# A graph layer on one Trainium2 core: aggregation by seven half-size products, and node loops in a written order

## The chip, the core and the metric

The kernel runs on one core of a Trainium2 chip. The core has five engines that run side by side: TensorE (PE, matrix products, with a weight loader of its own, PEld), VectorE (DVE), ScalarE (ACT), GpSimd (POOL) and SyncE (SP, which here only issues transfers). Each works through its own list of instructions in order and waits on semaphores for the others. TensorE writes its products to PSUM, eight banks of 128 x 512 fp32 numbers; VectorE and ScalarE read them from there; everything else lives in SBUF, and DMA moves data between SBUF and memory. The metric is the time of one execution on the device in microseconds (us), less being better.

## What is computed

For 32 graphs (batches) of 512 nodes with 256 features each, and a 0/1 matrix `adj` of 512 x 512 for each graph, one layer of a gated graph network, all in fp32:

```python
h = jnp.maximum(_layernorm(x), 0.0)
xc = jnp.transpose(h, (0, 2, 1))
t = relu(bn1(conv1d(xc, conv1_w)))               # 1 tap: a matrix product
t = bn2(conv1d(t, conv2_w, pad=8))               # 17 taps, 256 x 256 channels
x_conv = relu(t + xc).transpose(0, 2, 1)
s = h @ w_se.T + b_se                            # 3 numbers a node
A = jnp.exp(-squared_distance(s, s)) * adj
msg = relu(h @ w_msg.T + b_msg)
x_nmp = jnp.einsum('bnm,bmd->bnd', A, msg)       # the aggregation
gi = concatenate([x_conv, x_nmp]) @ w_ih.T + b_ih
gh = h @ w_hh.T + b_hh
r, z = sigmoid(gi_r + gh_r), sigmoid(gi_z + gh_z)
n = tanh(gi_n + r * gh_n)
out = x + (1 - z) * n + z * h
```

`A` is symmetric, since `adj` is.

## The kernel before

The batches are worked on in two groups (`g`) of 16. For each group `first_part` normalises, transposes (h goes to memory as `HD`), applies the 1-tap convolution and takes windows of 80 tokens to the frequency domain (`xf`). The 17-tap convolution is done there as 40 products by frequency, called units (`u`): unit 0 holds the two real frequencies, every other unit a complex number for each of 128 windows and 256 channels, times a 256 x 256 complex matrix. `load_unit` fetches the two matrices of a unit (`WT`, three buffers), `prepare` makes the sums that a complex product by three real ones needs (on GpSimd), and `product` multiplies, closes the sums and stores the result to memory (`YD`).

The function `nodes` follows each group's first part. It loops over the 16 batches of the group and does, for each, the following:

- `by_chunks` reorders h (ScalarE), `message` multiplies it by the message weights together with the three projection columns (TensorE; bias on VectorE, relu on ScalarE), `features` makes the small vectors from which a squared distance is one product (VectorE), `factors` transposes them (TensorE, copies by ScalarE).
- `affinity` multiplies the factors (tile `pd`), takes the exponent (`e`, ScalarE), transposes the 0/1 matrix in 32 x 32 blocks (`at`, VectorE) and multiplies the two into `A` (VectorE).
- `aggregate` multiplies the messages by `A`: two banks of 128 x 512 (tile `pn`), each a sum over four blocks of 128 nodes. ScalarE copies them to `nmp`, and `save_nmp` stores them to memory (`ND`).

The units are spread over the loop to fill TensorE: 36 of group 0 over its 16 iterations (two, two, two, three, and so on; the last four go into the first part of group 1), 40 of group 1 over the first 13 iterations (three each, four in the last). An iteration works ahead: it aggregates batch i, makes messages of batch i+2 and the affinity of batch i+1.

A late stage then reads HD, ND and YD back, takes the convolution back from the frequency domain (constant `back`, made on the host) and computes the gates. It takes about 965 us and isn't touched but for numbers in `back`. It already computes its gate products by seven half-size products out of sums that GpSimd makes (`sums`, tiles `hp`, `np`, `cp`).

The order of instructions on each engine is the order of the program text inside `tc.manual_schedule()`. Outside, a scheduler orders them by priority as they become ready in its own model of time. In `nodes` only the opening lines (988 to 993) stand inside such a block; the loop over the batches (995 to 1022) is left to the scheduler. Buffers are taken from pools, where tiles with one tag share `bufs` slots, and a new tile waits for the last reader of the one whose slot it takes. PSUM is one such pool of eight banks.

An fp32 product appears in the profile as two matmul instructions: the eight products of one aggregation are sixteen MATMULs.

Of the kernel before, what the change touches and what calls it, by code (L numbers as in the profile page):

```python
# [15 lines left out]
P = 128  # L16
# [14 lines left out]
def dft_constants(taps, tokens):  # L31
# [16 lines left out]
    back[2::2], back[3::2] = 2 * cos.T, -2 * sin.T  # L48
# [17 lines left out]
def gnn_layer(  # L66
# [42 lines left out]
    XP, HP, NP, CP, YT, RZ, NT, OUT = ({} for _ in range(8))  # L109
# [252 lines left out]
    def prepare(pw, g, u, xf):  # L362
        if (g, u) not in WT:
            load_unit(g, u)
        if u > 0:
            if (g, u) not in WSUM:
                sum_unit(pw, g, u)
            re, im = factors_of(xf, u)
            both = BOTH[g, u] = pw.tile([P, 2, DC, P], FP, tag="both", name=f"both_{g}_{u}", bufs=2)
            nc.gpsimd.tensor_tensor(both[:, 0], re, im, op=ALU.add)  # L370
            nc.gpsimd.tensor_tensor(both[:, 1], im, re, op=ALU.subtract)

    def product(pw, g, u, xf):
# [11 lines left out]
        else:  # L385
            both, wsum = BOTH.pop((g, u)), WSUM.pop((g, u))
            k3 = bank(f"py2_{g}_{u}")[:, :D]
            terms = [(k3, both[:, 1], wr), (k2, both[:, 0], wi), (k1, re, wsum)]
# [7 lines left out]
        else:  # L396
            nc.scalar.copy(y_im, halves(k1))  # L397
            nc.vector.tensor_sub(y_re, y_im, halves(k2))  # L398
            nc.vector.tensor_add(y_im, y_im, halves(k3))
        nc.scalar.dma_start(YD[g][:, 2 * u : 2 * u + 2, :], y)  # L400
# [67 lines left out]
    def affinity(b):  # L468
# [7 lines left out]
        for mc in range(NC):  # L476
            e = pools["nodes"].tile([P, N], FP, tag="e", name=f"e_{b}_{mc}", bufs=2)
            nc.scalar.activation(e, pd[mc], AF.Exp)  # L478
            at = pools["nodes"].tile([P, N], FP, tag="at", name=f"at_{b}_{mc}", bufs=2)
            nc.vector.transpose(at.rearrange("p (j k) -> p j k", k=32), ADJ[b][:, :, 32 * mc : 32 * (mc + 1)])  # L480
            nc.vector.tensor_mul(A[b][:, mc, :], e, at)  # L481
        del ADJ[b]

    def aggregate(b, dcs=range(DC)):
        if 0 in dcs:
            NMP[b] = work.tile([P, DC, N], FP, tag="nmp", name=f"nmp_{b}")
        for dc in dcs:
# [5 lines left out]
        if DC - 1 in dcs:  # L493
            del MSG[b], A[b]
# [441 lines left out]
    with tc.tile_pool(name="freq", bufs=1) as fpool:  # L936
# [36 lines left out]
        def nodes(g, xf, units, last):  # L973


            b1 = (g + 1) * GB
            todo = [b1 - 1] + list(range(g * GB, b1 - 1))
            def begin(i):
                if i < GB:
                    if todo[i] not in HQ:  # L980
                        by_chunks(todo[i])
                    message(todo[i])
                    features(todo[i])

            load_adj(todo[0])
            if (g, 2) not in WT:
                load_unit(g, 2)
            with tc.manual_schedule():
                begin(0)
                message(todo[1], [0])  # L990
                factors(todo[0])
                message(todo[1], [1])
                features(todo[1])
            affinity(todo[0])
            for i, b in enumerate(todo):
                mine = spread(units, i, last) if i < last else []
                more = i + 1 < GB
# [3 lines left out]
                if g + 1 < NG and i == 3 * GB // 4:  # L1001
                    statistics(b1)
                if more:
                    load_adj(todo[i + 1])
                    factors(todo[i + 1])

                parts = [range(DC)] if mine or not more else [[0], [1]]
                if len(parts) > 1:
                    aggregate(b, parts.pop(0))
                for u in mine[:1]:  # L1010
                    product(pools["pw"], g, u, xf)
                begin(i + 2)
                if i + 3 < GB:
                    load_h(todo[i + 3])
                if more:
                    affinity(todo[i + 1])
                for u in mine[1:2]:
                    product(pools["pw"], g, u, xf)
# [108 lines left out]
```

## Time and profile before

| | before |
|---|---|
| time, median of 3 runs | 1830.86 us (1827.69 to 1835.83) |
| span of the profiled execution, first to last instruction | 1830.0 us |
| time of the profiled execution beyond its span | not given apart |
| PE busy | 1815.0 us (99%) |
| DVE, ACT, POOL busy | 1107.4, 583.8, 588.6 us |
| loop of group 0 | about 157 to 460 us of the span |
| loop of group 1 | about 565 to 865 us |
| late stage | about 865 to 1830 us |

A group of instructions in the profile is one line of the kernel on one engine: the tiles written and read, the shape, the count, then busy time in us and the mean of one in ns, then the idle time of the engine ahead of it and what ended it. A timeline line gives the start in us, the length, the engine, the line and the tiles; "x16" stands for sixteen instructions merged. In a table of stretches, each engine has its busy time and its instructions.

### The profile page before, as it was taken

To read this page: it belongs to the slowest core of one execution; us is meant where nothing else is said; L and a number is where in the kernel's file an instruction comes from. 1 tells how busy PE (TensorE), PEld (TensorE's weight loads), DVE (VectorE), ACT (ScalarE), POOL (GpSimd) and SP (SyncE) were. 2 spreads that over 40 slices of the span, in tenths; PEclk is the share of its full clock that TensorE was granted. 3 is DMA by queue.
4 is the path that set the end of the run, shared out by engine and by line. 5 is a ranking of instruction groups with operands and counts; after the bars stand their busy time and mean duration, and the time that the engine had idled before them with its cause. 6 is when DMAs were issued, how large, how long until landed. Compare 5 with 4: busy or idle time off the path is not lost.

```text
span 1830.0 us, 20109 instructions
## 1 busy us (share of the span) xinstructions
PE 1815.0 (99%) x6614; PEld 1083.9 (59%) x6614; DVE 1107.4 (61%) x2220; ACT 583.8 (32%) x1084; POOL 588.6 (32%) x569
## 2 busy tenths in 40 slices
PE   9999999999999999999999999999999999999998
PEld 6777666666997766765545554555445554555444
DVE  7884565655995555554266556654665466645666
ACT  4555443432345343333212221222122221222121
POOL 3431333334432443444321332123221323133221
PEclk9999999999999999999999999999999999999999
DMA  9998989775669987767332344224422443234412
GB/s 252 307 297 220 254 225 263 192 197 190 214 218 226 262 242 226 237 187 256 93 108 57 77 121 121 78 44 121 121 87 35 120 121 98 51 93 121 114 23 54
DMA packets 308652, 289.26 MB, mean 158 GB/s; under 512 B 148076, under 2 KB 238732, under 8 KB 308164
## 3 DMA queue, kind: packets, MB, share of 16 engines
q1 hardware_dynamic: 282964, 225.79, 46.4%
q10 hardware_dynamic: 18992, 38.68, 5.9%
q0 software_dynamic: 6592, 23.50, 4.1%
q8 instruction: 53, 0.87, 0.2%
q14 instruction: 51, 0.42, 0.1%
HBM read 191.50 MB, written 96.40 MB: 157 GB/s over the span
## 4 chain that ended last, share of the span: by engine, by line
PE 65%; issue 1%; DVE 1%; POOL 1%; ACT 0%; DVEq 0%; POOLq 0%; ACTq 0%
PE pg L600 30%; PE pn L600 15%; PE pn L490 6%; PE py L391 6%; PE pc L588 5%; PE pm L438 2%; PE pd L475 1%; PE pz L600 1%; PE psr L464 0%; DVE A L481 0%; POOL cp L578 0%; POOL nt L791 0%; POOL rz L790 0%; DVE at L480 0%; DVE o L671 0%
## 5 line engine op out<-in xcount | busy, mean ns | idle before, releaser
L490 PE MATMUL pn<-A,msg 128*128 128x512 f32 x512 | 225.6, 593 | 0.9 <-DVE A L481 0.9
L600 PE MATMUL pg<-hp,sw 128*128 128x512 f32 x434 | 221.8, 593 | 0.7 <-DVE rz L619 0.5
L600 PE MATMUL pg<-np,sw 128*128 128x512 f32 x434 | 221.6, 592 | 0.0
L600 PE MATMUL pg<-cp,sw 128*128 128x512 f32 x434 | 221.6, 592 | 0.0
L578 POOL TENSOR_TENSOR hp<-hp 128x512 f32<-128x512 f32 x64 | 81.3, 1281 | 413.1 <-DMA hp<-hd 352.0
L370 POOL TENSOR_TENSOR both<-xf 128x256 f32<-128x256 f32 x78 | 60.1, 770 | 319.1 <-PE py L391 283.7
L490 PEld LDWEIGHTS pn<-A,msg 128*128 128x128 f32 x512 | 96.9, 190 | 111.0 <-issue 105.8
L578 POOL TENSOR_TENSOR cp<-cp 128x512 f32<-128x512 f32 x64 | 80.5, 1268 | 229.8 <-ACT cp L594 228.6
L391 PE MATMUL py<-wt,both 128*128 128x256 f32 x624 | 151.0, 384 | 0.5 <-ACT e L478 0.5
L615 ACT ACTIVATE rz<-rz,brz 128x512 f32<-128x512 f32 x93 | 67.0, 721 | 260.2 <-DVE rz L619 260.2
L398 DVE TENSOR_TENSOR y<-y,py 128x256 f32<-128x256 f32 x78 | 31.8, 407 | 188.5 <-ACT y L397 186.3
L600 PEld LDWEIGHTS pg<-hp,sw 128*128 128x128 f32 x434 | 82.2, 190 | 104.7 <-issue 97.3
L600 PEld LDWEIGHTS pg<-cp,sw 128*128 128x128 f32 x434 | 82.5, 190 | 103.8 <-issue 103.8
L600 PEld LDWEIGHTS pg<-np,sw 128*128 128x128 f32 x434 | 82.5, 190 | 103.8 <-issue 103.8
L391 PEld LDWEIGHTS py<-wt,both 128*128 128x128 f32 x624 | 113.9, 190 | 43.6 <-issue 27.6
L481 DVE TENSOR_TENSOR A<-e,at 128x512 f32<-128x512 f32 x128 | 115.7, 942 | 29.5 <-ACT e L478 29.3
L357 POOL TENSOR_TENSOR wsum<-wt 128x512 f32<-128x512 f32 x78 | 109.7, 1407 | 56.1 <-DMA wt<-wd 42.9
L739 ACT ACTIVATE nt<-nt,vech 128x512 f32<-128x512 f32 x64 | 46.2, 722 | 235.8 <-DVE nt L738 235.8
L326 PE MATMUL pc<-w,hT 128*128 128x256 f32 x512 | 118.9, 386 | 0.8 <-DVE hT L314 0.8
L438 PE MATMUL pm<-wmsg,hq 128*128 128x259 f32 x512 | 117.5, 381 | 0.0
L600 PE MATMUL pn<-cp,sw 128*128 128x512 f32 x224 | 114.4, 592 | 0.0
L600 PE MATMUL pn<-hp,sw 128*128 128x512 f32 x224 | 114.4, 592 | 0.0
(145 smaller groups left out, 2945.8 us busy)
## 6 DMA issues: line engine op xcount, KB each, us to landing
wt<-wd SPq DMA_DIRECT2D x160, 256.0 KB, 4.3
adj<-in_adj_dram SPq DMA_DIRECT2D x128, 256.0 KB, 5.4
wd<-wst SPq DMA_DIRECT2D x64, 320.0 KB, 5.9
yd<-y ACTq DMA_DIRECT2D x80, 256.0 KB, 3.9
yt<-yd SPq DMA_DIRECT2D x30, 640.0 KB, 7.5
hd<-hT SPq DMA_DIRECT2D x32, 512.0 KB, 5.0
nd<-nmp ACTq DMA_DIRECT2D x32, 512.0 KB, 4.5
xb<-in_x_dram SPq DMA_DIRECT2D x128, 128.0 KB, 3.7
```

The costliest lines, as they stand in the source:

```text
L326: nc.tensor.matmul(p[:, j, :], HT[b][:, ic, c * P : (c + 1) * P], w1[:, ic, :], start=(ic == 0), stop=(ic == DC - 1))
L357: nc.gpsimd.tensor_tensor(t, WT[g, u][:, 0], WT[g, u][:, 1], op=ALU.add)
L370: nc.gpsimd.tensor_tensor(both[:, 0], re, im, op=ALU.add)
L391: nc.tensor.matmul(dst, v[:, ic, :], w[:, ic, :], start=(ic == 0), stop=(ic == DC - 1))
L438: nc.tensor.matmul(p[:, : D + NS], hq[:, ic, c * P : (c + 1) * P], wmsg[:, ic, :], start=(ic == 0), stop=(ic == DC - 1))
L481: nc.vector.tensor_mul(A[b][:, mc, :], e, at)
L490: nc.tensor.matmul(p, MSG[b][:, mc, dc * P : (dc + 1) * P], A[b][:, mc, :], start=(mc == 0), stop=(mc == NC - 1))
L578: nc.gpsimd.tensor_tensor(t[:, dst, :], t[:, a, :], t[:, b, :], op=sub)
L588: nc.tensor.matmul(bk[:, t0:t1], YT[p][j][:, c, oc * P : (oc + 1) * P], back[:, n : n + t1 - t0], start=(c == 0), stop=(c == len(spans) - ...
L600: nc.tensor.matmul(bk[:, t], sw[:, k, q, o, :], terms[k][q][:, t], start=(first and i == 0), stop=(i == len(ks) - 1), skip_group_check=True)
L615: nc.scalar.activation(rz[:, g, j, :], src, AF.Sigmoid, bias=brz[:, g : g + 1], scale=1.0)
L739: nc.scalar.activation(n, n, AF.Tanh, bias=b_in[:, i : i + 1], scale=1.0)
```

## The change

**Aggregation.** For batches with `i <= last` (all 16 of group 0, the first 14 of group 1) `aggregate7` replaces `aggregate`. The 256 x 512 by 512 x 512 product is cut into 2 x 2 blocks and done by seven half-size products of sums instead of eight (Strassen's scheme in Winograd's form). Each is four MATMUL of 256 columns over two contraction blocks, twice for fp32. The sums of `A`'s blocks (`affinity_sums`, tile `ts`) and of the messages' blocks (`message_sums`, tile `ms`) are made by GpSimd, four instructions each. Three PSUM banks are used; products accumulate into a bank after ScalarE has copied what stood there, and VectorE closes the four output blocks with five additions.

**Affinity.** `affinity` becomes three functions: `turn` (the transposes), `exponents` (the exponent goes straight to `A`, without `e`), and `masked` (the multiplication, in place).

**Complex products.** `prepare` makes one sum of the data (`re + im`) instead of a sum and a difference. ScalarE writes one product twice, once multiplied by -2, so that the stored second part is imaginary minus real; `back` is changed to match. The order of the three terms is turned around, and the store can be put off (`later`).

**Order.** Both calls of `nodes` stand wholly in `tc.manual_schedule()`. Loads of units follow the products, 0/1 matrices are loaded two batches ahead, and stores of products are collected and issued by `flush`.

**Buffers.** `nmp` one instead of two; `e` goes; `ts` and `ms` one each; `p7` two; `both` half as large.

```diff
-    back[2::2], back[3::2] = 2 * cos.T, -2 * sin.T
+    back[2::2], back[3::2] = 2 * (cos - sin).T, -2 * sin.T
...
-            both = BOTH[g, u] = pw.tile([P, 2, DC, P], FP, tag="both", name=f"both_{g}_{u}", bufs=2)
-            nc.gpsimd.tensor_tensor(both[:, 0], re, im, op=ALU.add)
-            nc.gpsimd.tensor_tensor(both[:, 1], im, re, op=ALU.subtract)
+            both = BOTH[g, u] = pw.tile([P, DC, P], FP, tag="both", name=f"both_{g}_{u}", bufs=2)
+            nc.gpsimd.tensor_tensor(both, re, im, op=ALU.add)
...
-            terms = [(k3, both[:, 1], wr), (k2, both[:, 0], wi), (k1, re, wsum)]
+            terms = [(k1, re, wr), (k2, im, wi), (k3, both, wsum)]
...
-            nc.scalar.copy(y_im, halves(k1))
-            nc.vector.tensor_sub(y_re, y_im, halves(k2))
+            nc.scalar.copy(y_re, halves(k1))
+            nc.scalar.mul(y_im, halves(k1), -2.0)
+            nc.vector.tensor_sub(y_re, y_re, halves(k2))
             nc.vector.tensor_add(y_im, y_im, halves(k3))
-        nc.scalar.dma_start(YD[g][:, 2 * u : 2 * u + 2, :], y)
+        store = partial(nc.scalar.dma_start, YD[g][:, 2 * u : 2 * u + 2, :], y)
...
+    def turn(b, mcs):
+        for mc in mcs:
+            at = AT[b, mc] = pools["nodes"].tile([P, N], FP, tag="at", name=f"at_{b}_{mc}", bufs=2)
+            nc.vector.transpose(at.rearrange("p (j k) -> p j k", k=32), ADJ[b][:, :, 32 * mc : 32 * (mc + 1)])
...
-            e = pools["nodes"].tile([P, N], FP, tag="e", name=f"e_{b}_{mc}", bufs=2)
-            nc.scalar.activation(e, pd[mc], AF.Exp)
...
-            nc.vector.tensor_mul(A[b][:, mc, :], e, at)
+            nc.scalar.activation(A[b][:, mc, :], pd[mc], AF.Exp)
+
+    def masked(b, mcs):
+        for mc in mcs:
+            nc.vector.tensor_mul(A[b][:, mc, :], A[b][:, mc, :], AT.pop((b, mc)))
+
+    H = N // 2
+
+    def quads(t, width):
+        return [t[:, 2 * k : 2 * k + 2, width * j : width * (j + 1)] for k in range(2) for j in range(2)]
+
+    def affinity_sums(b):
+        b11, b12, b21, b22 = quads(A[b], H)
+        t = TS[b] = pools["nodes"].tile([P, 3, 2, H], FP, tag="ts", name=f"ts_{b}", bufs=1)
+        sub = ALU.subtract
+        nc.gpsimd.tensor_tensor(t[:, 0], b22, b12, op=sub)
+        nc.gpsimd.tensor_tensor(b12, b12, b11, op=sub)
+        nc.gpsimd.tensor_tensor(t[:, 1], b22, b12, op=sub)
+        nc.gpsimd.tensor_tensor(t[:, 2], b21, t[:, 1], op=sub)
+
+    def message_sums(b):
+        a11, a21, a12, a22 = quads(MSG[b], P)
+        t = MS[b] = pools["nodes"].tile([P, 3, 2, P], FP, tag="ms", name=f"ms_{b}", bufs=1)
+        sub = ALU.subtract
+        nc.gpsimd.tensor_tensor(t[:, 0], a11, a21, op=sub)
+        nc.gpsimd.tensor_tensor(a21, a21, a22, op=ALU.add)
+        nc.gpsimd.tensor_tensor(t[:, 1], a21, a11, op=sub)
+        nc.gpsimd.tensor_tensor(t[:, 2], a12, t[:, 1], op=sub)
...
+    def aggregate7(b):
+
+        m11, s1, m12, m22 = quads(MSG.pop(b), P)
+        b11, t1, b21, b22 = quads(A.pop(b), H)
+        (s3, s2, s4), (t3, t2, t4) = ([t[:, n] for n in range(3)] for t in (MS.pop(b), TS.pop(b)))
+        nmp = NMP[b] = work.tile([P, DC, N], FP, tag="nmp", name=f"nmp_{b}", bufs=1)
+        c11, c12, c21, c22 = (nmp[:, i, H * j : H * (j + 1)] for i in range(2) for j in range(2))
+        p1 = pools["nodes"].tile([P, H], FP, tag="p7", name=f"p7_{b}", bufs=2)
+
+        def add_product(bk, left, right, first):
+            for k in range(2):
+                nc.tensor.matmul(bk, left[:, k, :], right[:, k, :], start=(first and k == 0), stop=(k == 1),
+                                 skip_group_check=True)
+
+        x, y, z = (bank(f"pn{k}_{b}")[:, :H] for k in range(3))
+        add_product(x, m11, b11, True)
+        nc.scalar.copy(p1, x)
+        add_product(y, s2, t2, True)
+        nc.scalar.copy(c12, y)
+        add_product(z, s1, t1, True)
+        nc.scalar.copy(c21, z)
+        add_product(x, m12, b21, False)
+        nc.scalar.copy(c11, x)
+        add_product(y, s3, t3, False)
+        nc.scalar.copy(c22, y)
+        nc.vector.tensor_add(c12, c12, p1)
+        nc.vector.tensor_add(c22, c22, p1)
+        nc.vector.tensor_add(c22, c22, c21)
+        add_product(z, s4, b22, False)
+        nc.vector.tensor_add(c12, c12, z)
+        add_product(y, m22, t4, False)
+        nc.vector.tensor_add(c21, p1, y)
...
+            def multiply(u):
+                product(pw, g, u, xf, stores)
+                if u + 2 in units:
+                    prepare(pw, g, u + 2, xf)
+                load_units(1)
+
             load_adj(todo[0])
...
+            load_adj(todo[1])
+            load_units(3 - sum((g, u) in WT for u in units))
+            load_h(todo[3])
+            message(todo[0])
+            features(todo[0])
+            message(todo[1], [0])
+            factors(todo[0])
+            message(todo[1], [1])
+            turn(todo[0], [0, 1])
+            features(todo[1])
+            exponents(todo[0])
+            by_chunks(todo[2])
+            masked(todo[0], [0, 1])
+            turn(todo[0], [2, 3])
+            masked(todo[0], [2, 3])
+            affinity_sums(todo[0])
+            prepare(pw, g, units[1], xf)
             for i, b in enumerate(todo):
                 mine = spread(units, i, last) if i < last else []
...
+                if len(more) > 1:
+                    load_adj(more[1])
+                if len(more) > 3:
+                    load_h(more[3])
+                if seven:
+                    message_sums(b)
                 if more:
...
+                    factors(more[0])
+                flush()
                 for u in mine[:1]:
...
+                    multiply(u)
+                if len(more) > 1:
+                    message(more[1])
+                    flush()
+                    features(more[1])
                 if more:
...
+                    turn(more[0], [0, 1])
+                    exponents(more[0])
+                    masked(more[0], [0, 1])
                 for u in mine[1:2]:
...
+                    multiply(u)
+                if more:
+                    turn(more[0], [2, 3])
+                    masked(more[0], [2, 3])
+                if seven:
+                    aggregate7(b)
+                else:
+                    aggregate(b)
+                if more and i + 1 <= last:
+                    affinity_sums(more[0])
+                flush()
+                for u in mine[2:]:
+                    multiply(u)
                 save_nmp(b)
...
+                if len(more) > 2:
+                    by_chunks(more[2])
+            flush()
```

`more` holds the next four batches of the group. `load_units` issues the next loads of a list that for group 0 also holds the first two of the four units left for later.

## The prediction

> **What bounds the kernel now.** I read the page first, then busy time by stretch, then TensorE's own timeline in the node loops, and last the durations of the engines to which the change gives work. From the page:
>
> ```profile
> PE 1815.0 (99%) x6614; PEld 1083.9 (59%) x6614; DVE 1107.4 (61%) x2220; ACT 583.8 (32%) x1084; POOL 588.6 (32%) x569
> L490 PE MATMUL pn<-A,msg 128*128 128x512 f32 x512 | 225.6, 593 | 0.9 <-DVE A L481 0.9
> L391 PE MATMUL py<-wt,both 128*128 128x256 f32 x624 | 151.0, 384 | 0.5 <-ACT e L478 0.5
> L481 DVE TENSOR_TENSOR A<-e,at 128x512 f32<-128x512 f32 x128 | 115.7, 942 | 29.5 <-ACT e L478 29.3
> L357 POOL TENSOR_TENSOR wsum<-wt 128x512 f32<-128x512 f32 x78 | 109.7, 1407 | 56.1 <-DMA wt<-wd 42.9
> ```
>
> TensorE (PE) is never free; the others have a third to two thirds left. The aggregation (L490) holds 225.6 us of it. [...]Busy time of each engine over the two node loops:
>
> ```profile
> core 0: us, PE busy (x) PEld busy (x) DVE busy (x) ACT busy (x) POOL busy (x), PEclk, DMA share, GB/s
> 179.00:460.00 281.00, 280.73 (x1110) 185.50 (x1109) 160.21 (x399) 105.97 (x212) 108.29 (x114) 1.00 0.77 217
> 584.00:836.00 252.00, 252.00 (x1017) 171.59 (x1016) 137.31 (x338) 92.79 (x190) 105.07 (x111) 1.00 0.79 226
> ```
>
> PE is full in both; GpSimd (POOL) works 39 and 42% there, VectorE (DVE) 57 and 54%, ScalarE (ACT) 37%. One iteration, from TensorE's timeline:
>
> ```profile
> 204.57 0.27 PE L459 MATMUL psl<-ident,fl 128*128 128x128 f32 x1
> 204.68 0.60 PE L464 MATMUL psr<-ident,fr 128*128 128x128 f32 x4
> 205.12 1.89 PE L391 MATMUL py<-wt,both 128*128 128x256 f32 x8
> 206.85 1.03 PE L391 MATMUL py<-wsum,xf 128*128 128x256 f32 x4
> 207.71 3.67 PE L438 MATMUL pm<-wmsg,hq 128*128 128x259 f32 x16
> 211.31 1.14 PE L475 MATMUL pd<-sr,sl 9*128 9x512 f32 x8
> 212.38 1.99 PE L391 MATMUL py<-wt,both 128*128 128x256 f32 x8
> 214.22 1.03 PE L391 MATMUL py<-wsum,xf 128*128 128x256 f32 x4
> 215.08 7.03 PE L490 MATMUL pn<-A,msg 128*128 128x512 f32 x16
> 221.94 0.27 PE L459 MATMUL psl<-ident,fl 128*128 128x128 f32 x1
> ```
>
> Starts follow each other without a hole. factors takes 0.55 us, a product 2.59 (205.12 to 207.71), a message 3.60, the exponents 1.07, an aggregation 6.86 (215.08 to 221.94). Aggregations start every 17.37 us with two products, every 19.96 with three.
>
> [...]6.86/16 = 429 ns with 512 columns, 2.59/12 = 216 with 256. [...]The timeline of all engines shows it:
>
> ```profile
> 605.46 0.71 POOL L370 TENSOR_TENSOR both<-xf 128x256 f32<-128x256 f32 x1
> 605.50 2.35 DVE L481 TENSOR_TENSOR A<-e,at 128x512 f32<-128x512 f32 x2
> 606.14 1.17 POOL L371 TENSOR_TENSOR both<-xf 128x256 f32<-128x256 f32 x1
> 622.13 1.29 DVE L481 TENSOR_TENSOR A<-e,at 128x512 f32<-128x512 f32 x2 [0.68 <-ACT e L478]
> ```
>
> Two L481 take 1.29 us alone and 2.35 against POOL; a POOL sum grows from 0.73 to 1.17.[...]
>
> **The change, part by part.**
>
> *Seven products.* Sixteen 512-column instructions become 28 of 256 columns: 28 x 0.216 = 6.05 us against 6.86, 0.82 saved. It holds for 16 batches of the first loop and 14 of the second (i <= last): 30 x 0.82 = **24.6 us**. The matmuls of `product` stay 12 with the same shapes.
>
> *POOL.* Affinity sums are four 128x512 at 1.27 (hp, L578, min 1.26) = 5.1 us; message sums four 128x256 at 0.73 = 2.9; preparing a unit falls from 2.7 to 1.27 + 0.73 = 2.0. The first loop's two-product iteration then has 12.0 us against a new PE period of 17.37 - 0.82 = 16.55; the second's three-product one 14.0 against 19.14. Collisions: at most 0.45 per VectorE operation with two SBUF inputs, seven of these a batch, 3.2 us: 15.2 and 17.2, still below. What matters is when. `ts` and `ms` have one buffer, so affinity sums of the next batch wait until the last product of this one ends (E): E to E+5.1; then (after one prepare, in three-product iterations) message sums, the needed s2 being third: E+7.3 or E+9.3. PE wants it for the second of the seven, at E+0.55+2.59+3.60+1.07+2.59+0.86 = E+11.3, or E+13.9. Cover 4 us; hidden.
>
> *DVE.* The five closing additions cost about 5 x 0.4 (y, 0.41) = 2.0 us. Pairs of transposes and of L481 start 1.2 us apart. From the message's end on PE (E+6.7): its last addition +0.7, features 0.45, two transposes 1.2, two masks 1.2, the pair for y 0.8, transposes 1.2, masks 1.2: E+13.5 to 15 with collisions, while the seven end at E+16.55. So the last addition lands 0.6 to 1.1 us after E'.
>
> *ACT.* One 0.37 more per product, five copies of 0.37 instead of two of 0.585, exponents the same. save_nmp waits on ACT for that last addition, and by_chunks (2 x 0.6) is queued behind it; PE's next message waits for by_chunks: ready at E'+2.3, wanted at E'+3.1. Free, with 0.8 us of cover. Inside the seven, the last product overwrites nothing but needs ACT's copy of bank y: y's second product drains at 4.5 us, copied at 4.9; PE's weight load wants it at 5.0. I charge 0.05 each: **-1.5**.
>
> *Starts.* All is now by hand, with turn ahead of features and affinity sums ahead of the first unit's prepare. Second loop, before's times: exponents end 573.5; features end 575.0 behind two transposes, so PE waits 1.5 for psl; masks end 579.2, affinity sums 584.3, both 585.1; PE reaches the third term at 583.7 and waits 1.4; s2 another 0.5. First aggregation at 586.0 plus 0.5 instead of 584.18: **-2.3**. The first loop likewise, where the adjacency lands later and wsum must be made too (2.0 instead of 0.73): 182.2 instead of 179.07, **-3.1**. In its second iteration before lost 1.3 (18.64 for 17.37), which goes: **+1.3**.
>
> *Ends.* The first loop's last iteration has only 5.2 us of products ahead of the seven, s2 comes at 7.3 against 6.0: **-1.5** with the collision. At the second loop's end the 0.9 wait at L490 goes (a whole plain aggregation now covers the masks), but the exponents of the last batch wait for sl and sr behind save_nmp: **+0.9 - 0.9**.
>
> *Moved loads and stores.* On SP load_adj and load_h run an iteration earlier, load_unit follows each product and waits for the slot that this product frees; a unit takes 4.3 us to land and is next touched by POOL a product later: hidden, and the bytes moved are the same. If the cover failed, prepare would wait up to 7 us (the longest such wait shown) once. y's stores move behind already finished additions. `nmp` with one buffer: its store (4.5 us) is out long before the next copy at E+12. New tile addresses could delay the late stage's first loads: 0 to 3 us, I take 0.
>
> Sum: 24.6 - 1.5 - 2.3 - 3.1 + 1.3 - 1.5 = 17.5. Against the profiled span, 1830.0 - 17.5 = 1812.5; the span is 0.9 below the median of the three times, so 1830.9 - 17.5 = **1813**. The back constants cost nothing at run time.
>
> **Rivals.** (a) The DVE-to-ACT chain fails: more collisions make the closing addition late beyond E'+1.9, by_chunks then stalls the message. The first loop's two-product iterations have 0.8 us of cover, so 2 us late costs 1.2 x 12, or about 0.4 a batch over both loops: 1813 + 12 = **1825**. For it: [...]POOL is twice as busy. Against: before's L481 at its mean of 0.94 instead of 0.6 adds only 1.4.
> (b) Slower: POOL's chain E to s2. It decides where a batch loses 17.5/30 = 0.6 us, which is a chain of 11.9 us instead of 7.3, a stretch of 1.6 on every step. A single 0.73 sum was seen stretched by 1.6, a 1.27 one by 1.35. With 1.8 the chain is 13.1, 1.8 lost in 30 batches, 54 - 17.5: **1867**. Against: DVE has 3.5 us of such operations a batch, too few to stretch 8 us so far; for: a strided two-row form on POOL is not in the trace, and may cost more than the plain one.
> (c) It doesn't do what it says: two 256-column matmuls cost more than one 512 with the new waits between groups of four. At no saving, the starts and ends alone remain: **1838**. Against: L391 already runs so, at 216 ns.
>
> **Chances.** My sum 0.60 (1806 to 1820); better still, if the starts hide, 0.04 (below 1806); (a) 0.20 (1819 to 1830), a third of it beyond 0.5%; (c) 0.03; (b) 0.13. Half a per cent, 9 us, is about what a measurement tells from no change here. Faster 0.60 + 0.04 + 0.07 = 0.71; same 0.13 + 0.03 = 0.16; slower 0.13. The range 1806 to 1834 leaves 0.04 below and 0.16 above; the likeliest case's own is 1806 to 1820.
>
> **What would show it.** Right: 16 pn matmuls become 28 in about 6.05 us, aggregations start 16.55 or 19.14 us apart, PE full between; POOL near 70% in the loops; holes of 2 to 3 us at the loops' starts. Wrong: PE waiting before pm on ACT hq (a), before pn on POOL ms or ts (b), or 28 matmuls taking 6.9 us (c); a wait on ACT's copies inside every group of seven would cost 30 times itself.

## The result, and the profile after

The changed kernel takes 1826.42 us (median of 4 runs, 1823.95 to 1829.15) against 1831.26 for the kernel before in the same measurement: a ratio of **0.9973** (95% interval 0.9955 to 0.9992). It is faster by a quarter of a per cent, less than the half per cent that I had named as the bound, and 13 us above the forecast. Ten further runs of it gave 0.9976 (0.9967 to 0.9985). The profiled span went from 1830.0 to 1825.1 us.

The lines of the page that answer to those of before, from the profile after:

```profile
PE 1793.3 (98%) x6974; PEld 1152.5 (63%) x6974; DVE 1203.6 (66%) x2370; ACT 617.9 (34%) x1252; POOL 781.1 (43%) x731
L357 POOL TENSOR_TENSOR wsum<-wt 128x512 f32<-128x512 f32 x78 | 107.6, 1380 | 83.3 <-DMA wt<-wd 57.7
L492 DVE TENSOR_TENSOR A<-A,at 128x512 f32<-128x512 f32 x128 | 108.2, 882 | 1.9 <-ACT A L488 1.9
```

PE works 21.7 us less (1815.0 before), but the span is only 4.9 us shorter: PE now stands idle for 31.8 us where it stood idle for 15.0. Busy time by stretch of the kernel after, the same two stretches as before:

```profile
179.00:460.00 281.00, 275.58 (x1329) 226.11 (x1328) 208.24 (x488) 123.37 (x298) 218.57 (x207) 0.99 0.76 216
584.00:836.00 252.00, 252.00 (x1227) 208.66 (x1226) 190.00 (x428) 114.61 (x278) 194.42 (x190) 1.00 0.82 230
```

The columns are as in the prediction's table. PE has holes of 5.4 us in the first loop and none in the second; POOL is at 78 and 77% (39 and 42% before). One iteration of the kernel after, from TensorE's timeline:

```profile
402.12 0.27 PE L463 MATMUL psl<-ident,fl 128*128 128x128 f32 x1
...
412.63 1.03 PE L538 MATMUL pn<-A,msg 128*128 128x256 f32 x4
413.49 1.03 PE L538 MATMUL pn<-ts,ms 128*128 128x256 f32 x4
414.36 1.89 PE L538 MATMUL pn<-A,msg 128*128 128x256 f32 x8
...
417.81 1.03 PE L538 MATMUL pn<-ts,msg 128*128 128x256 f32 x4
418.67 0.27 PE L463 MATMUL psl<-ident,fl 128*128 128x128 f32 x1
```

The seven products take 418.67 - 412.63 = 6.04 us from start to start, and the iteration 16.55: the steady state is what the sum had. (The mean of one on a page is no such price: 593 ns for the plain products of 512 columns, whose starts lie 429 ns apart.) The loss shows where PE waits. Its chief waits in the kernel after (us in total, times, longest):

```profile
PE psl L463 <- DVE fl L456: 11.6, 2, 8.9
PE pn L538 <- POOL ms L514: 3.5, 3, 2.2
PE pm L442 <- ACT hq L427: 1.9, 3, 1.0
...
PE pd L486 <- ACT sr L470: 1.2, 1, 1.2
```

Two waits for `psl`, one at the start of each loop, stand for more than all others here. Cut at marks that both TensorE timelines share (a mark is the start of an instruction), the 4.9 us come from:

| stage | before | after | change | the forecast's terms |
|---|---|---|---|---|
| start to first message of loop 0 | 157.69 | 156.07 | -1.62 | 0 |
| to its first aggregation | 21.38 | 29.94 | **+8.56** | +3.1 |
| to its 16th aggregation | 260.77 | 251.99 | -8.78 | -12.85 |
| to the next part's first transpose | 9.46 | 12.74 | **+3.28** | +0.73 |
| to the first message of loop 1 | 115.49 | 114.71 | -0.78 | 0 |
| to its first aggregation | 19.39 | 23.01 | **+3.62** | +1.8 |
| to the late stage | 280.51 | 270.91 | -9.60 | -10.28 |
| late stage | 965.31 | 965.73 | +0.42 | 0 |
| sum | 1830.0 | 1825.1 | -4.90 | -17.5 |

One profile of each kernel stands behind the table. In a second profile of the kernel after, the first four rows are 157.44, 29.37, 255.67 and 10.77 us, and the two of loop 1 are 23.85 and 269.28. Both starts come back within 0.9 us; the gain in the first row is chance, and the other rows move by 1.6 to 3.7 us.

The start of loop 0, in the timeline of the kernel after:

```profile
172.16 1.30 DVE L475 STREAM_TRANSPOSE at<-adj 128x512 f32<-128x512 f32 x2 [7.83 <-DMA adj<-in_adj_dram]
...
173.78 0.48 PE L463 MATMUL psl<-ident,fl 128*128 128x128 f32 x1 [8.91 <-DVE fl L456]
...
174.95 3.62 PE L390 MATMUL py<-wt,xf 128*128 128x256 f32 x8
```

`turn` waits 7.83 us on DVE for the 0/1 matrix, `features` stands behind it, and PE waits 8.91 us for `features`. Then the eight matmuls of the first unit take 3.62 us, where eight of them take 1.89 in the loop. In the kernel before, the same transposes come later and wait for nothing, and the first unit is slow as well:

```profile
168.62 3.25 PE L391 MATMUL py<-wt,xf 128*128 128x256 f32 x8
...
176.29 1.31 DVE L480 STREAM_TRANSPOSE at<-adj 128x512 f32<-128x512 f32 x2
```

So the wait is what is new: this second `psl` starts 10.00 us after the loop's first message before and 17.71 after, which is 7.71 of the 8.56 us; 0.85 come behind it. In loop 1 the times are 8.73 and 11.48, 2.75 of the 3.62 us. A second chain runs beside PE's in the kernel after and is as late. POOL makes `both` for the first complex unit behind the masks and the affinity sums, and ends 0.3 us before PE reads it:

```profile
184.10 0.74 POOL L370 TENSOR_TENSOR both<-xf 128x256 f32<-128x256 f32 x1
...
185.15 1.03 PE L390 MATMUL py<-wsum,both 128*128 128x256 f32 x4
```

### The profile page after: what moved, and what is told of

It is laid out like the page before. It is cut to its first block, busy times and chain, and to the rows that moved or that the text cites. A ratio compares the mean times of both kernels' runs of the same rounds, so it can differ in the third digit from the quotient of the medians.

```text
span 1825.1 us, 21215 instructions
## 1 busy us (share of the span) xinstructions
PE 1793.3 (98%) x6974; PEld 1152.5 (63%) x6974; DVE 1203.6 (66%) x2370; ACT 617.9 (34%) x1252; POOL 781.1 (43%) x731
## 4 chain that ended last, share of the span: by engine, by line
PE 92%; DVE 2%; POOL 2%; issue 2%; DMA 1%; ACT 0%; SPq 0%; ACTq 0%; DVEq 0%; POOLq 0%
PE pg L664 30%; PE pn L664 15%; PE py L390 11%; PE pn L538 9%; PE pm L442 6%; PE pc L326 6%; PE pc L652 5%; PE px L341 3%; PE pd L486 2%; PE pw L254 2%; PE phT L310 1%; DMA adj<-in_adj_dram 1%; PE pn L522 1%; PE pz L664 1%; PE psr L468 1%
## 5 line engine op out<-in xcount | busy, mean ns | idle before, releaser
L390 PE MATMUL py<-wt,xf 128*128 128x256 f32 x640 | 157.0, 389 | 0.0
L390 PEld LDWEIGHTS py<-wt,xf 128*128 128x128 f32 x640 | 118.6, 193 | 35.4 <-issue 21.2
L664 PE MATMUL pn<-np,sw 128*128 128x512 f32 x224 | 114.4, 592 | 0.0
L326 PEld LDWEIGHTS pc<-w,hT 128*128 128x128 f32 x512 | 94.6, 190 | 23.9 <-issue 5.6
L492 DVE TENSOR_TENSOR A<-A,at 128x512 f32<-128x512 f32 x128 | 108.2, 882 | 1.9 <-ACT A L488 1.9
L442 PEld LDWEIGHTS pm<-wmsg,hq 128*128 128x128 f32 x512 | 97.0, 191 | 19.0 <-ACT hq L427 4.0
L652 PEld LDWEIGHTS pc<-back,yt 128*128 128x128 f32 x640 | 92.7, 190 | 7.7 <-issue 7.7
```

Of the source, the lines that this page charges most:

```text
L326: nc.tensor.matmul(p[:, j, :], HT[b][:, ic, c * P : (c + 1) * P], w1[:, ic, :], start=(ic == 0), stop=(ic == DC - 1))
L390: nc.tensor.matmul(dst, v[:, ic, :], w[:, ic, :], start=(ic == 0), stop=(ic == DC - 1))
L442: nc.tensor.matmul(p[:, : D + NS], hq[:, ic, c * P : (c + 1) * P], wmsg[:, ic, :], start=(ic == 0), stop=(ic == DC - 1))
L492: nc.vector.tensor_mul(A[b][:, mc, :], A[b][:, mc, :], AT.pop((b, mc)))
L652: nc.tensor.matmul(bk[:, t0:t1], YT[p][j][:, c, oc * P : (oc + 1) * P], back[:, n : n + t1 - t0], start=(c == 0), stop=(c == len(spans) - ...
L664: nc.tensor.matmul(bk[:, t], sw[:, k, q, o, :], terms[k][q][:, t], start=(first and i == 0), stop=(i == len(ks) - 1), skip_group_check=True)
```

## The experiments

The expectations call the theories by letters. **Q**: VectorE's queue (features behind a turn that waits for the matrix) is the loss at the starts. **C**: POOL's chain, masks, affinity sums, then prepare, then message sums, would set the first aggregation anyway. **V**: with the first batch aggregated plainly, VectorE's queue (a message's additions behind the masks) is next. **S**: SP's order of loads is what is late at the start. **H**: the half rate of the first products there comes from TensorE's idling. All ratios are to the kernel before on the same chip; "third end" is the time in loop 0 from the first message to the end of the third aggregation, "to first" that to the start of the first, from each run's TensorE timeline. A period, or an iteration's time below, goes from the end of one aggregation to the end of the next.

| run | ratio (95%) | median us | loop 0 to first | loop 0 third end | loop 1 to first |
|---|---|---|---|---|---|
| before | 1 | | 21.38 | 64.25 | 19.39 |
| after | 0.9973 (0.9955-0.9992) | 1826.42 | 29.94 | 71.15 | 23.01 |
| after, again | 0.9976 (0.9967-0.9985) | 1826.93 | 29.37 | 70.74 | 23.85 |
| order alone | 1.0079 (1.0067-1.0091) | 1845.50 | 29.76 | 71.36 | 24.86 |
| features first | 1.0004 (0.9996-1.0012) | 1832.14 | 31.29 | 75.00 | 23.84 |
| prepare first | 0.9999 (0.9990-1.0008) | 1831.77 | 26.53 | 73.15 | 18.97 |
| filler | one run | 1826.58 | 29.73 | 70.23 | 22.47 |
| first plain | 0.9952 (0.9938-0.9965) | 1822.29 | 27.45 | 68.47 | 18.98 |
| masks behind | 0.9972 (0.9966-0.9979) | 1826.37 | 18.98 | 70.58 | 18.98 |
| last plain | 0.9958 (0.9944-0.9972) | 1823.89 | 18.98 | 70.88 | 18.97 |
| matrix first | 0.9975 (0.9968-0.9983) | 1826.57 | 25.69 | 70.41 | 23.65 |
| loads only | 0.9985 (0.9977-0.9993) | 1828.65 | 29.43 | 73.50 | 23.41 |
| reorder early | 0.9963 (0.9949-0.9976) | 1824.58 | 29.45 | 69.50 | 23.14 |
| unit load ahead | 0.9934 (0.9922-0.9946) | 1819.53 | 18.98 | 67.72 | 18.98 |
| all edits | 0.9909 (0.9896-0.9922) | 1815.21 | 24.57 | 66.50 | 18.98 |
| all but matrix first | 0.9932 (0.9919-0.9945) | 1819.47 | 19.74 | 68.77 | 18.98 |

**The order without the seven products.** Everything else of the change stays.

```diff
-            affinity_sums(todo[0])
-                seven = i <= last
+                seven = False
-                if more and i + 1 <= last:
+                if False:
                     affinity_sums(more[0])
```

> Edit: the changed kernel with the plain aggregation for every batch and without the sums on GpSimd; the fixed order, the complex products and the buffers stay. If the seven products are worth 0.82 us a batch and the rest of the change costs what the starts show, the aggregations start 17.37 and 19.96 us apart again, psl still waits about 9 and 2.7 us behind the matrix, and the time is 1835 to 1843, slower than the kernel before. If the order itself had gains that the starts hide, it stays at or below 1831.

It is slower than before by 0.8%, 14 us, and 2.5 us above the range that was expected. The periods are 17.37 and 19.96 us, those of the kernel before; PE waits 8.95 and 3.4 us for `psl`, and the two first aggregations are late by 8.4 and 5.5 us. So the seven products are worth the step from 1.0079 to 0.9973, 19 us, and the loss at the starts comes with the rest of the change, without any sum of theirs on POOL. Which part of that rest (order, loads, form of the complex product, buffers) is told apart below only for order and loads.

**Features ahead of the transposes.**

```diff
-            turn(todo[0], [0, 1])
             features(todo[1])
+            turn(todo[0], [0, 1])
```

> Edit: in the opening of each loop the two transposes of the 0/1 matrix stand behind the features of the second batch on VectorE instead of ahead of them. Theory Q (queue): TensorE lost its time at the starts because features, and with them psl, stood behind a transpose that waited for the 0/1 matrix. Then the 8.9 and 2.7 us waits at psl go and the time falls by 8 to 11 us, to about 1816. Theory C (chain): the first seven products can't start before matrix, masks, affinity sums, prepare and message sums are through, one after the other, however early psl is. Then the waits at psl go, TensorE waits instead before the third term of the first complex product on POOL both, the first aggregation starts at the same place after the loop's first message (29.9 and 23.0 us before, now within 1 us), and the time stays within 2 us of 1826.

Both waits for `psl` are gone, and nothing is won: the first aggregation of loop 0 comes 1.35 us later still, and the whole is some 5 us slower than the kernel after. TensorE's timeline of this run, from the first complex unit on:

```profile
179.50 3.75 PE L390 MATMUL py<-wt,xf 128*128 128x256 f32 x8 [5.29 <-issue]
...
187.28 2.07 PE L390 MATMUL py<-wsum,both 128*128 128x256 f32 x4 [4.03 <-POOL both L370]
```

PE is through the message sooner. It then stands 5.29 us until VectorE, behind the masks that wait for the matrix, comes to the third message's additions (178.91; "masks behind", below, shows this link), and 4.03 us for `both`, which POOL makes behind the affinity sums; the eight matmuls behind the first of these waits take 3.75 us, at about half the rate of the loop (1.89). Q names the wait rightly but not the cause of the loss. C has the place of the first aggregation (in loop 1 it moves by 0.84 us) and the wait for `both`, but neither the wait of 5.29 us nor the time, which lies 4 us above its range.

**The unit's prepare ahead of the affinity sums**, on top of the last edit.

```diff
-            affinity_sums(todo[0])
             prepare(pw, g, units[1], xf)
+            affinity_sums(todo[0])
```

> Edit: as the run with features first, and GpSimd prepares the first complex unit before it makes the affinity sums. Theory C: the complex product no longer waits; the wait moves once more, to the second of the seven products, on POOL ms; since prepare (2.0 us in the first loop, 0.75 in the second) leaves the chain, 2 to 5 us are won in all: about 1822. Theory Q: no further gain over the run before it (1816 by that theory).

The first aggregation starts sooner (26.53 and 18.97 us after the message), but now its second product waits: `pn` for `ms` on POOL, 12.0 us in five waits over the kernel. The second iteration takes 21.11 us. In loop 1 the second aggregation starts 24.57 us after the first instead of 19.14. At 1831.77 us both theories miss: C had 1822, Q 1816. The chain has only changed its last link.

**Keeping PE warm.** 36 matmuls that nobody reads (10 in loop 1) are put behind the exponents; the rest is the kernel after.

```diff
             exponents(todo[0])
+            fb = bank(f"fill_{g}")[:, :D]
+            for _ in range(18 if g == 0 else 5):
+                nc.tensor.matmul(fb, ident, back[:, :D], start=True, stop=True)
```

> Edit: the changed kernel, with 36 matmul instructions of 256 columns on constants (10 in the second loop) put on TensorE behind the first exponents, where it otherwise stands idle 8.9 and 2.7 us; they write a bank that nobody reads. Theory H: after those waits the products ran at half rate because TensorE had been idle; filled, the eight matmuls of unit 0 take 1.7 to 1.9 us instead of 3.4 to 3.6 and 3.0, though the fillers add work, and the first aggregation starts no later. If the half rate has another cause (late operands), they stay at 3 us and more.

From TensorE's timeline of this run:

```profile
165.90 8.04 PE L1075 MATMUL fill<-back,ident 128*128 128x256 f32 x36
...
175.55 1.89 PE L390 MATMUL py<-wt,xf 128*128 128x256 f32 x8
...
185.94 1.13 PE L390 MATMUL py<-wsum,both 128*128 128x256 f32 x4 [1.99 <-POOL both L370]
```

The eight matmuls of the first unit take 1.89 us again (3.62 in the kernel after; 1.89 for 3.03 in loop 1). H holds there, but the time saved is waited out 8 us later for `both`: the start is no shorter (29.73 and 22.47 us). At the start of loop 0 half rate costs nothing: what is late is POOL (a wait of 1.99 us for `both`), not PE.

**The first batch of each loop by the plain aggregation**, with features and prepare first; its affinity sums fall away.

```diff
-            affinity_sums(todo[0])
-                seven = i <= last
+                seven = 0 < i <= last
```

> Edit: features first, prepare first, and the first batch of each loop with the plain aggregation, so that no sum on GpSimd stands between the 0/1 matrix and TensorE there. Theory C: the first aggregation starts about 21 us after the loop's first message in the first loop (masks then end about 21 us after it) and 18.5 in the second, 8 and 4 us sooner than in the changed kernel; two batches lose 0.82: about 1815. Theory Q: the same as with features first alone, plus 1.6: about 1818 or more.

This wins: 0.9952, though not the 1815 of theory C. Loop 1 starts in 18.98 us, below the 19.39 of before. Loop 0 takes 27.45, where 21 was expected. Here VectorE does the four transposes and masks of the first batch behind an 8.09 us wait for the matrix, and the additions of the third message stand behind them until 178.93; PE waits 5.8 us at `py` (179.52), and the next run asks whether it is for the PSUM banks of that message.

**Masks of the first batch behind the third message's additions**, on top of that.

```diff
-            turn(todo[0], [0, 1])
...
-            masked(todo[0], [0, 1])
-            turn(todo[0], [2, 3])
-            masked(todo[0], [2, 3])
...
                     features(more[1])
+                if i == 0:
+                    for mcs in ([0, 1], [2, 3]):
+                        turn(b, mcs)
+                        masked(b, mcs)
```

> Edit: first batch plain, features and prepare first, and now the first batch's transposes and masks stand on VectorE behind the additions and features of the loop's third message instead of ahead of them. In the run with the first batch plain, TensorE still waited 5.8 us ahead of the first complex product. Theory V (VectorE's queue): that wait is for PSUM banks which the additions of the third message free, and these stand behind masks that wait for the 0/1 matrix. Then the 5.8 us go, the first aggregation starts 20 to 22 us after the loop's first message instead of 27, and the time falls by 4 to 7 us against the run with the first batch plain, to 0.992 of the kernel before. Theory D (data): the wait is for the unit's matrices by DMA; then it stays and nothing is won.

As V says, that wait is gone, and loop 0 aggregates after 18.98 us, 2.4 sooner than before. But the second iteration takes 28.11 us, where it took 17.27 with the last edit. From the timeline of all engines of this run:

```profile
189.96 9.11 SPq L353 DMA_DIRECT2D wt<-wd  x4
...
199.59 1.26 POOL L357 TENSOR_TENSOR wsum<-wt 128x512 f32<-128x512 f32 x1 [10.86 <-DMA wt<-wd]
...
209.90 2.08 PE L538 MATMUL pn<-ts,ms 128*128 128x256 f32 x4 [4.53 <-POOL ms L514]
```

POOL stands 10.86 us for the matrices of the next unit, which SP issues from 189.96 on, behind the third batch's 0/1 matrix and the load of h; and the affinity and message sums stand behind `wsum`. Whole, the kernel is 4 us slower than with the last edit, where V had it 4 to 7 faster.

**The last batch of loop 0 plain as well.**

```diff
-                seven = 0 < i <= last
+                seven = 0 < i <= min(last, GB - 2)
```

> Edit: as the run with the masks behind, and the last batch of the first loop is plain too. Theory: the last batch's seven products waited 2.2 us for POOL ms and then ran about 1.8 us slower; a plain aggregation costs 0.8 more and waits for nothing: 2 to 3.5 us less than the run with the masks behind, about 0.9905. If the slow stretch after the wait had another cause than the wait, at most 1.4 us are won.

2.5 us less (1826.37 to 1823.89). The tail of loop 0, from its last `psl` to the next part's first transpose, falls from 30.35 to 28.79 and so shows 1.6 of it; the intervals of the two ratios overlap a little.

**Order of loads.** First the 0/1 matrix of the first batch ahead of the first two units (in the kernel after), then, on the kernel "last plain", the next unit ahead of the second iteration's matrix and h, then this alone in the kernel after.

```diff
-                for u in range(2):
-                    load_unit(0, u)
...
             load_adj(todo[0])
+            load_units(2 - sum((g, u) in WT for u in units))
             load_adj(todo[1])
```

> Edit: the changed kernel, in which the first loop loads its first 0/1 matrix ahead of units 0 and 1 on SP instead of behind them (1 MB that queues ahead of it). Theory: the chain at the first loop's start hangs on the landing of that matrix; it lands about 4 us sooner, psl's wait of 8.9 us shrinks to about 5, and the seven products start 3 to 5 us sooner: 0.995. If the matrix is late for another cause (its own descriptors, the memory its tile takes over), nothing moves.

```diff
-                if len(more) > 1:
+                if i > 0 and len(more) > 1:
                     load_adj(more[1])
-                if len(more) > 3:
+                if i > 0 and len(more) > 3:
                     load_h(more[3])
...
                     multiply(u)
+                if i == 0:
+                    load_adj(more[1])
+                    load_h(more[3])
```

> Edit: as the run with the last batch plain, and in the first iteration the loads of the next 0/1 matrix and of h stand behind the first product, so that the load of unit 3 is issued ahead of them on SP. In that run the wait had moved into the second iteration: POOL stood 10.9 us at wsum for unit 3, whose load was queued on SP behind a matrix that waited for its buffer, and the sums of the second batch stood behind wsum. Theory S (SP's queue): the first message to the second iteration's end shrinks from 54.3 us to 47 to 49 in the first loop, POOL's wait for that unit falls below 4 us, the second loop wins 1 to 2 us: 0.9915. Theory B (bandwidth alone): DMA is full there, another transfer is late in its place, and at most 2 us are won.

> Edit: the changed kernel, in which only the order of loads in the first iteration is altered as in the run with the unit's load ahead. Theory S and C together: with the seven products of the first batch still behind matrix, masks and sums, the first aggregation stays where it is, and only the second iteration gains, 0 to 1.5 us: 0.9965 to 0.9975.

The first starts loop 0 4.3 us sooner (25.69) and loses it in the second iteration (21.21). The whole wins nothing, where 0.995 was expected. The second brings that iteration from 28.11 to 17.64, but the third takes 24.17, with 5.3 us of waiting for `ms` behind the next late unit: 0.9934, 4.4 us less than "last plain", of which the third end shows 3.2. Loop 1, where S had 1 to 2 us more, wins nothing: its first aggregation stays at 18.98 us. The third edit, in the kernel after, wins nothing either (1828.65, some 2 us more, and the third end 2.4 us later): the chain through POOL's sums is late there whatever the loads do. S holds where the first batch is plain, and only partly.

**by_chunks ahead of save_nmp**, in the kernel after: rival (a) taken away.

```diff
-                save_nmp(b)
                 if len(more) > 2:
                     by_chunks(more[2])
+                save_nmp(b)
```

> Edit: the changed kernel with by_chunks ahead of save_nmp on ScalarE, nothing else. In the changed kernel single iterations of the first loop are longer than 16.55 us (17.58 and 17.18 in its first profile, 20.8 in its second), where closing additions collide with GpSimd's sums and the reordering of h stands behind them. Theory A (collision and queue): these iterations go back to 16.55 and 2 to 4 us are won: 0.9955. If the late thing is not the closing addition, the long iterations stay.

All iterations of loop 0 between the first and the last two take 16.55 or 19.14 us, and these thirteen 222.88 us instead of 225.85 and 228.45 in the two profiles of the kernel after. The kernel takes 1824.58, some 2 us less than after. The intervals of the ratios overlap, and it is one profile against two: "masks behind" and "unit load ahead" have no long iteration behind their third either, without this edit. What the edit removes, in the timeline of the kernel after:

```profile
197.08 3.86 PE L442 MATMUL pm<-wmsg,hq 128*128 128x259 f32 x16 [0.96 <-ACT hq L427]
...
261.35 1.49 DVE L552 TENSOR_TENSOR nmp<-nmp,p 128x256 f32<-128x256 f32 x1
...
266.22 1.14 ACT L427 COPY hq<-hT 128x512 f32<-128x512 f32 x2 [4.47 <-DVE nmp L558]
...
266.89 3.85 PE L442 MATMUL pm<-wmsg,hq 128*128 128x259 f32 x16 [0.68 <-ACT hq L427]
```

The first closing addition takes 1.49 us, where it takes 0.41 alone, while POOL is preparing a unit; the next two take 0.95 and 1.37. ACT waits for the last at save_nmp, by_chunks follows, and PE waits 0.68 us. The same happens in the second iteration (197.08), with 0.96 us.

**All edits together**: first and last batch plain, masks behind, the two load orders, by_chunks first; then the same without the matrix first.

> Edit: as the run with the unit's load ahead, plus the first 0/1 matrix ahead of units 0 and 1, and by_chunks ahead of save_nmp on ScalarE. Theory: the first removes what is left of the wait for the matrix (0 to 3 us), the second the stalls of the message behind the closing additions (1 to 4 us in the first loop, where single iterations were 0.6 to 4 us longer than 16.55): 0.989. If both are hidden by then, no change against the run before it.

> Edit: the run with all edits without the first 0/1 matrix ahead of units 0 and 1. Tells which of its two additions won the 4 us against the run with the unit's load ahead. If by_chunks did it, the time stays at 0.991 of the kernel before and the first loop has no iteration above 17 us; if the matrix did, it is back at 0.9935 with a long second or third iteration.

The whole is the fastest kernel of the study, 1815.21 us, **0.9909** (0.9896 to 0.9922). Every iteration of loop 0 between the first and the last two takes 16.5 to 16.8 or 19.14 us. Taking the matrix-first edit out again costs 4.3 us (1819.47), though it makes the first aggregation sooner (19.74 against 24.57): the third iteration goes back to 23.94. (The intervals of the two ratios just touch.) Against "unit load ahead", by_chunks first adds nothing that can be told (0.9932 and 0.9934).

## Where the prediction failed, and what of it was right

**Seven products, 24.6: right.** Periods fell from 17.37 to 16.55 and from 19.96 to 19.14, 0.82 each. Beside "order alone" they bring 17.2 us of span: 24.6 less what they lose at the end and in single iterations of loop 0.

**ACT, -1.5: nothing.** The seven take 6.04 us in the loop, against 28 x 0.216 = 6.05.

**Starts, -3.1 and -2.3: this step failed.** They cost 8.56 and 3.62 us, 12.2 instead of 5.4 (4.9 without the half microsecond behind the first product). I saw that features stands behind the transposes, and priced it with their duration: a wait of 1.5 us for `psl`. It was 8.91 us in loop 0 and 2.68 in loop 1. What the sum put at nothing is the time at which the matrix lands. For loop 0 I wrote that it lands later and didn't ask when. The chain of the kernel after answers: in flight until 172.04, so that a turn which the kernel before runs at 176.29, with its data landed, now waits 7.83 us, with all of VectorE's queue behind it (and 1.61 in loop 1). The load itself is no later: its last part lands 16.5 us after the loop's first message before (174.23) and 16.0 after.

The trace of the kernel before would have given the start of loop 0. To these 16.5 us come, by my own durations, four pairs of transposes and masks (4.8), features (0.45), the affinity sums (5.1), `wsum` and `both` (2.0) and the third term (0.86): an estimate of 29.7 us to the first aggregation. The forecast had 24.5; 29.94 was measured.

A second cost was left out, half rate: behind some of PE's waits, the shortest of 1.01 us, the granted clock is 0.50 for a while. Stretches of the kernel after, TensorE's granted clock in the third column from the right:

```profile
174.00:177.00 3.00, 3.00 (x10) 2.60 (x10) 3.00 (x6) 0.85 (x2) 0.00 (x0) 0.50 1.15 227
...
441.00:444.00 3.00, 2.82 (x8) 2.32 (x9) 0.82 (x1) 0.37 (x1) 2.92 (x5) 0.63 0.49 170
```

It explains little of the loss at the start of loop 0, since the kernel before pays it there too (3.25 us for its first eight matmuls, granted clock 0.50 from 167.9 to 171.4 us, after a wait of 1.01 us). In loop 1 only the kernel after does (3.03 instead of 1.89).

Nor is the wait for `psl` the whole of it, since its removal didn't shorten the start. The experiments found several links, each with about the same lateness behind it: VectorE's queue, POOL's sums, the banks that the third message's additions free, the next unit's load. A first aggregation by seven products needs all four masks and 8 us of sums; a plain one starts with the first block. That is why 0.9952 came with the plain first batch and 0.9999 without.

**Moved loads, hidden: wrong at the starts, right in the loop.** PE waits for no load in the steady state. POOL does at `wsum` (11 times in loop 1, 41.3 us between 600 and 830, where it was 15.8 before), without PE waiting for it. At the start of loop 0 the DMA engines are full (share 1.07 in the kernel before and 1.09 after, 158 to 178 us), and SP's order decides what lands late: once VectorE's queue was mended, POOL waited 10.86 us for a unit. "Up to 7 us once" was the cost without cover; there it is more, and the wait is POOL's before it is PE's.

**+1.3 for the second iteration of before: not won.** It takes 17.86 in the kernel after, 1.31 above the period. PE waits there for `hq` behind the closing additions, which is rival (a); with by_chunks first it takes 16.55, and in "order alone", without closing additions, 17.37, the period of before.

**Ends, -1.5: right in its cause, off in its size.** The message sums come late as foreseen:

```profile
441.18 1.55 PE L538 MATMUL pn<-ts,ms 128*128 128x256 f32 x4 [2.15 <-POOL ms L514]
```

The wait was 2.15 us instead of 1.3, and most of the matmuls behind it ran at half rate (441.18 to 445.56 for twelve instead of 2.6 us). The end lost 4.1 us of which 3.3 show beside the 0.82 won. In the second profile the wait is 1.88 us, the twelve matmuls take 2.7 us (445.38 to 448.07), and 1.3 us show: the half rate came in one profile of two. At the end of loop 1, `pd` waited 1.2 us for ACT, as foreseen (0.9). The two plain aggregations behind this wait took 15.70 us in the one profile of the kernel after and 14.00 in the other:

```profile
843.84 15.70 PE L522 MATMUL pn<-A,msg 128*128 128x512 f32 x32
...
847.35 14.00 PE L522 MATMUL pn<-A,msg 128*128 128x512 f32 x32
```

**Rivals.** (a) was there, in single iterations instead of all: some 3 us in loop 0, which "reorder early" doesn't have. That the time came out where (a) had placed it (1825) is chance; most of the loss lay at the starts. (b) didn't come: POOL ended its sums in time in every iteration but the first and the last two of loop 0, although at 77% busy, and a sum over two rows took the 1.27 us that I had assumed (177.58). (c) neither. The sign and the wide range (1806 to 1834) held, the likeliest range (1806 to 1820) didn't, and by the bound of half a per cent the outcome was "no change", to which I had given 0.16.

**Open.** In the best kernel loop 0 still starts 24.57 us after its first message, with 3.2 us of waiting for the first unit. Whether full DMA engines or the order of the loads limits it wasn't told apart: no run moved fewer bytes there. How much of the 14 us of "order alone" belongs to the new form of the complex product or to the buffers wasn't tried; the two starts hold 12.6 of them (7.1 to the third end of loop 0 and 5.5 in loop 1).

## What to carry to other kernels

Where an instruction is moved ahead in an engine's written order, price it by the time at which its data lands, not by its duration (here a wait of 7.83 us ahead of two transposes that take 1.30 together); a trace in which it waits for nothing says only that it came late enough. At the starts here several things were late by about as much, so removing one wait was worth nothing until its successors were on time: compare the end of the second or third iteration, not the wait. And a scheme that saves in the steady state may be left out of the first and last rounds, where its preparation has nothing to hide behind.

## What the runs showed of the hardware that I had not expected

- TensorE's granted clock is at half for short stretches, and one can begin when PE is back at work. In the trace's records of it, the kernel after goes to 0.50 at 168.687, 441.753, 578.286 and 844.525 us, for 10.24 us the first time and for 3.41 the other three. Of these, the falls at 441.753 and 844.525 come 0.57 and 1.76 us after PE has started again (441.18, 842.77). The kernel before goes to 0.50 at 27.998 and 167.945, for 3.41 us each. A last stretch in each trace (from 1820.737 and 1826.822) is cut off by the end of the kernel. The falls named lie 273.066, 136.533 and 266.239 us apart in the kernel after and 139.947 in the kernel before, which is 80, 40, 78 and 41 times the 3.413 us of the shortest stretches.
- The length of a wait didn't decide it here. Waits of 1.01 us (kernel before, to 166.42), 1.16 (to 842.77) and 2.15 us (to 441.18) were followed by half rate. Three others were not, by the times of the matmuls behind them: 1.16 us at the same place in the second profile, 1.88 us there, and 1.99 in the filler run. With the filler matmuls in the long wait, the granted clock stayed at 1.00 from 165.9 to 182 us (1.89 us for eight matmuls instead of 3.62). What decides it the runs don't tell.
- The very small instructions of `features` stretch too: the 128 x 12 copy (L456) has a median of 176 ns and a longest of 1209 ns, at 182.95, while POOL makes `wsum` (182.85 to 184.14).
